# A router in two steps and the order of three small products in a four-layer kernel

## Chip, cores and metric

The kernel runs on one core of a Trainium2 chip. Times are microseconds of that core for one execution. The runs of the kernel before took 614.46, 614.35 and 614.35 us; their median, 614.35 us, is the time that the prediction is about.

## What is computed

The input x is 8 sequences of 256 tokens with 1024 features. Four layers follow, each added to its own input. The first is the one that the change is in: a dense matrix, a router that picks the best two of eight experts for each token, and their rank-16 adapters weighted by the router's gates. The reference, cut to its lines:

```python
# layer 0
base = einsum('btd,od->bto', x, W)
logits = einsum('btd,ed->bte', x, Wr) + 5.0 * one_hot(language_ids, E)[:, None, :]
topw, topi = top_k(logits, 2)
weights = softmax(topw, axis=-1)
gates = sum(one_hot(topi, E) * weights[..., None], axis=-2)
h = einsum('btd,erd->bter', x, A)
x = x + base + 2.0 * einsum('bter,bte,eor->bto', h, gates, B)
# layer 1: W, bias and a +-1 mask of each sequence, scaled by its coefficient
x = x + (x @ W1.T + b1) + (x @ (2 * mask - 1)) * coeff
# layer 2: one of eight matrices for each sequence
x = x + einsum('bsi,boi->bso', x, weight[ids])
# layer 3: one of eight rank-16 adapters for each sequence
x = x + einsum('bnr,bor->bno', einsum('bni,bri->bnr', x, B3[ids]), A3[ids])
```

## The kernel before, in words

**Precision.** Each fp32 operand is used as the sum of a high part (a cast to fp32r on ScalarE, `highs`, L288) and a low part (the operand less its high part, on VectorE, `lows`, L68). A product is then three matmuls: high by high, high by low, low by high. The adds of the residual (x + x W) are folded into the matrices, as an identity added to their diagonal blocks on GpSimd (L235).

**Stages.** The sequences are taken in pairs (512 tokens), and two pairs make a group. For each of the two groups g, layer 0 runs first, over both pairs at once, with Strassen's scheme in Winograd's form (seven products instead of eight; one place in the order of eight is used for expert products, below). Then layers 1 and 2 run pair by pair in 32 unit slots each, and layer 3 is spread as filler between them and the next group.

**Slots of layer 0.** Layer 0 has 16 slots, two for each entry of the product list. A slot s is issued by `l0_slot` (L786), always in this order:

1. stores and one load that is due;
2. `l0_evacuate` (L727), which takes finished accumulators out: at s = 6 ScalarE copies C11, in two halves (L734); at s = 8 VectorE makes V = accumulators + U1, in two halves (L736);
3. works listed under -s;
4. the high parts of the operands of the slot after the next (`highs`, ScalarE), then low parts of the next slot (`lows`, VectorE);
5. works listed under s in `l0_works` (L662);
6. TensorE's own work, `l0_main` (L759).

Each engine takes its instructions in the order in which these calls issue them. High parts live in five buffers and low parts in four, so the casts of a slot wait until TensorE has ended with an operand of an earlier slot. The accumulators of the products are four banks in two tiles. A new chain starts at slots 0, 6 and 10 in the same two tiles, so slot 6 has to wait for the copy of C11, and slot 8, which goes on in the accumulators that V reads, for V.

**The router.** For a pair p (p0 is the second of the group, p1 the first) it goes like this. `logits` (L301) multiplies x with the router's weights on TensorE, and ScalarE copies the result. `by_token` (L315) transposes it on TensorE. `router` (L323) is a row of small VectorE operations: the sum of four partial results, the bias, the best logit and its expert, the second best and its expert, their difference d; then ScalarE takes the exponential of d (L357), and VectorE turns it into the two weights and multiplies them into the one-hot rows. `expand` (L371) repeats each gate over the 16 ranks. `gates_by_rank` (L380) transposes that on TensorE, four matmuls, and ScalarE copies it (L389). `gate` (L398) multiplies it with the expert products h, which `experts` (L612) has made on TensorE. `split_gates` (L391) makes ghi (ScalarE, L394) and glo (VectorE). `lora` (L622) then adds the adapters' products to the accumulators: three matmuls for each of four blocks m.

In the first group, p0 has its logits and transposes in the first two slots. Its router and expansion are works of slot 2, its gate transposes are in the middle of slot 3, `gate` is in slot 4, and `split_gates` opens slot 5. Slots 4 and 5 hold the expert products of p1 in place of a Strassen product, and slot 5 ends with `lora` for p0. For p1 the logits are in the middle of slot 3, `by_token` at its end, router and expansion in slot 5, gate transposes in the middle of slot 6, and the rest in slot 8; `lora` runs again in slots 9, 13 and 15. In the second group the router has been run for both pairs at once in a slot of layer 2, before that group starts (`side`, L941), and only `expand` is left for slots 2 and 5.

The lines that a sentence can't give:

```python
        evacuate()                      # l0_slot, L795
        l0_evacuate(g, s)
...
        highs(f + HI_AHEAD)             # HI_AHEAD = 4, two operands per slot
...
        lows(f + LO_AHEAD)              # LO_AHEAD = 3
        for work in w.get(s, []):
            work()
...
        if s in (0, 6, 10):             # l0_main, L764
            chain(g, s)
...
            product(s, g, range(2), start=(s in (0, 6, 10)), lora=part, mid=mid)
```

Of the kernel before, what the change touches and what calls it, by code (L numbers as in the profile page):

```python
# [8 lines left out]
F32 = mybir.dt.float32  # L9
# [6 lines left out]
P = 128  # L16
# [18 lines left out]
def kernel(ctx: ExitStack, tc: tile.TileContext, x, lang, coeff, ids,  # L35
# [31 lines left out]
    def tt(o, a, b, op):  # L67
        nc.vector.tensor_tensor(o, a, b, op)  # L68
# [246 lines left out]
    def by_token(p):  # L315
        pts[p] = bank(1 - p % 2, f"pt{p}")
        lg = lgs.pop(p)
        for n in range(4):
            nc.tensor.transpose(pts[p][:, n * P:(n + 1) * P], lg[:, n * P:(n + 1) * P], ident)

    gxs = {}

    def router(pairs):  # L323
        n4 = 4 * len(pairs)
        t = lambda nm, w: gp.tile([P, n4, w], F32, tag=nm, name=nm)
        lv = t("lv", E)
        for i, p in enumerate(pairs):
            quarters = pts.pop(p).rearrange("p (n g e) -> p n e g", n=4, g=4)[:, :, :E, :]
            nc.vector.tensor_reduce(
                lv[:, 4 * i:4 * i + 4].rearrange("p n (e o) -> p n e o", o=1), quarters, AX.X,  # L330
                ALU.add)
        b0, nb = 2 * pairs[0], 2 * len(pairs)
        lv4 = lv.rearrange("p (b h) e -> p b h e", h=2)
        tt(lv4, lv4, bias[:, b0:b0 + nb].rearrange("p b (o e) -> p b o e", o=1)
           .to_broadcast([P, nb, 2, E]), ALU.add)
        revb = rev.to_broadcast([P, n4, E])

        def top(v, nm):
            mx = t(f"mx{nm}", 1)
            nc.vector.tensor_reduce(mx, v, AX.X, ALU.max)  # L340
            eq = t(f"eq{nm}", E)
            tt(eq, v, mx.to_broadcast([P, n4, E]), ALU.is_equal)
            tt(eq, eq, revb, ALU.mult)
            fi = t(f"fi{nm}", 1)
            nc.vector.tensor_reduce(fi, eq, AX.X, ALU.max)
            oh = t(f"oh{nm}", E)
            tt(oh, revb, fi.to_broadcast([P, n4, E]), ALU.is_equal)
            return mx, oh

        m1, oh1 = top(lv, "1")  # L350
        rest = t("rest", E)
        nc.vector.scalar_tensor_tensor(rest, oh1, -3.0e38, lv, ALU.mult, ALU.add)
        m2, oh2 = top(rest, "2")
        d = t("d", 1)
        tt(d, m2, m1, ALU.subtract)
        ex = t("ex", 1)
        nc.scalar.activation(ex, d, AF.Exp)  # L357

        den = t("den", 1)
        nc.vector.tensor_scalar(den, ex, 1.0, 0.5, ALU.add, ALU.mult)  # L360
        wt1 = t("wt1", 1)
        nc.vector.reciprocal(wt1, den)
        wt2 = t("wt2", 1)
        tt(wt2, wt1, ex, ALU.mult)
        tt(oh1, oh1, wt1.to_broadcast([P, n4, E]), ALU.mult)
        tt(oh2, oh2, wt2.to_broadcast([P, n4, E]), ALU.mult)
        tt(oh1, oh1, oh2, ALU.add)
        for i, p in enumerate(pairs):
            gxs[p] = oh1[:, 4 * i:4 * i + 4, :]

    def expand(p):  # L371

        gx = gp.tile([P, 4 * E, R], F32, tag="lg", name=f"gx{p}", bufs=3)
        nc.vector.tensor_copy(gx, gxs[p].rearrange("p n (e o) -> p (n e) o", o=1)
                              .to_broadcast([P, 4 * E, R]))
        gxs[p] = gx
# [3 lines left out]
    def gates_by_rank(p):  # L380

        pg = bank(1 - p % 2, f"pg{p}")
        gx = gxs.pop(p)
        for n in range(4):
            nc.tensor.transpose(pg[:, n * P:(n + 1) * P],
                                gx[:, n * E:(n + 1) * E, :].rearrange("p e r -> p (e r)"),
                                ident)
        gts[p] = gp.tile([P, N], F32, tag="lg", name=f"gt{p}", bufs=3)
        copy(gts[p], pg)  # L389
# [200 lines left out]
    def link(*args, **kw):  # L590

        mm(*args, skip_group_check=True, **kw)  # L592
# [29 lines left out]
    def lora(p, w):  # L622
        def part(m, o, stop=False):
            hi, lo = gates[p]
            link(o, w[0](m), hi, start=False, stop=False)
            link(o, w[0](m), lo, start=False, stop=False)
            link(o, w[1](m), hi, start=False, stop=stop)
        return part

    def lb_half(i):  # L630
# [31 lines left out]
    def l0_works(g):  # L662


        p0, p1 = pair_of(g, 0), pair_of(g, 1)
        w = {}

        def at(s, *fs):
            w.setdefault(s, []).extend(fs)

        def add(name, h, src):
            nc.gpsimd.dma_start(quad(g, name)[h], src, accum_op=ALU.add)

        def s1_add(h):
            fold_quad(quad(g, "S1")[h], h)
            add("S1", h, w0[1, 2 + h])

        def s3_add(h):
            t = quad(g, "S3")[h]
            copy(flat(t), flat(quad(g, "S2")[h]))  # L680
            fold_quad(t, h)
            add("S3", h, w0[1, 2 + h])

        def s4_add(h):
            copy(flat(quad(g, "S4")[h]), flat(quad(g, "S2")[h]))
            add("S4", h, w0[0, 2 + h])

        def less(h, name, j, i):

            t = flat(quad(g, name)[h])  # L690
            nc.scalar.mul(t, t, -1.0)  # L691
            add(name, h, x[pair_of(g, j)][:, 4 * i + 2 * h:4 * i + 2 * h + 2])

        def both(f, *args):
            return [lambda h=h: f(h, *args) for h in range(2)]

        def subs(o, a, b):
            return [lambda h=h: sub(g, o, a, b, h) for h in range(2)]

        def lb_parts():  # L700
            copy(lbs[0], lb_raw)
            tt(lbs[1], lb_raw, f32(lbs[0]), ALU.subtract)

        if g == 0:
            at(1, constants, *both(s1_add))
            at(2, *both(less, "T1", 1, 0), lambda: router([p0]), lambda: expand(p0))
            at(3, lb_parts, *subs("S2", "A11", "S1"))
            at(4, *both(s4_add), lambda: gate(p0))
            at(5, lambda: router([p1]), lambda: expand(p1))
        else:  # L710
            at(0, *both(s1_add), *both(less, "T1", 1, 0))
            at(2, lambda: expand(p0))
            at(3, *subs("S2", "A11", "S1"))
            at(4, *both(s4_add), lambda: gate(p0))
            at(5, lambda: expand(p1))
        at(-5, lambda: split_gates(p0, gts[p0]))
        at(4, *both(less, "T3", 1, 1))
        at(7, *subs("T2", "T1", "B22"))
        at(7, *both(s3_add))
        at(8, lambda: gate(p1), lambda: split_gates(p1, gts[p1]), lambda: gate_difference(g))  # L720
        for h in range(2):
            at(9 + h, lambda h=h: add("T4", h, x[p0][:, 4 + 2 * h:6 + 2 * h]))
        for i in range(4):
            at(12 + i, lambda i=i: split_c(p1, i))
        return w
# [20 lines left out]
    def l0_mids(g):  # L746


        p0, p1 = pair_of(g, 0), pair_of(g, 1)
        if g == 0:  # L750
            return {3: lambda: [gates_by_rank(p0), logits(p1)()], -3: lambda: by_token(p1),
                    6: lambda: gates_by_rank(p1)}
        mids = {0: lambda: proj_pair(1, 0), 1: lambda: rank_pair(1, 1, (0, 1)),
                2: lambda: gates_by_rank(p0), 6: lambda: gates_by_rank(p1)}
        mids.update({s: lambda: fill(2) for s in (3, 4, 5)})
        mids[-5] = lambda: fill(2)
        return mids
# [151 lines left out]
    def side(n):  # L909

        kind, q, m, j = slots[n]
        if kind == "L1":
            return
        u = pos[slots[n]] % 16
        b = 2 * q
        if q % 2 == 0:
            if u < 2:
                load_l3(b + u)
            if u in (4, 5):
                prep_l3(b + u - 4)  # L920
            if u in (2, 5, 8, 11):
                split_c(q + 1, u // 3)
            return
        l, p = ((9, 10), (11, 12)) if q == 1 else ((4, 5), (9, 10))
        if u in l:
            load_l3(b + u - l[0])
        if u in p:
            prep_l3(b + u - p[0])
        if q == 1:
            if u == 0:  # L930
                X[1] = region(GX[1], "x1", [P, 2, K, N], F32)
            if u in (1, 3, 5, 7):
                k = 4 * (u // 2 % 2)
                load_x(1, u // 4, k, k + 4)
            if u == 10:
                LA[1] = place_la(2)
                nc.sync.dma_start(LA[1], la)
            if u in (12, 13):
                la_parts(1, 4 * (u - 12), 4 * (u - 12) + 4)
            if u == 15:  # L940
                router([2, 3])  # L941

    def unit_slot(n):
        kind, q, m, j = slots[n]
# [169 lines left out]
```

## Time and profile before

| What | Value |
|---|---|
| median of 3 runs | 614.35 us |
| the profiled execution's own time | 613.21 us |
| its span in the profile | 611.0 us |
| mean granted TensorE clock | 0.994 |
| matmuls | 3244, busy 597.0 us |
| small products of the gates, layer 0, both groups | 32 with ghi and 16 with glo in each group |
| layer 0, first group, slots 2 to 15 | about 23 to 119 us |
| layer 0, second group | about 305 to 413 us |

Engines are PE (TensorE matmuls), PEld (its weight loads), DVE (VectorE), ACT (ScalarE), POOL (GpSimd) and SP (SyncE, which issues most DMAs). L12 is line 12 of the kernel. Tiles appear under the program's names: `whi` and `wlo` are high and low parts of operands, `mm` the accumulators of layer 0, `c` the blocks C11 to C22 and U1, V, W between them, `A` and `x` the Strassen operands, `pl`, `pt`, `pg`, `ph` the logits, their transposes, the gates' transposes and the expert products, `d` and `ex` the router's difference and its exponential, `gx` the expanded gates. The busy rows of the page show a slice of 15.3 us as one digit, in tenths, so that 9 means 90% or more. A wait is given as: engine, tile and line of the waiting instruction, what released it, then total us, number of times, and the longest. L68 is the helper of all two-operand VectorE work, and so is told apart by its tiles. Matmuls overlap: one of 512 columns is shown with 0.39 us but the next starts some 0.23 us after it, so positions are read from starts.

### The profile page before, as it was taken

What the parts mean: (1) busy time and instruction counts of PE and PEld (TensorE: products, weight loads), DVE (VectorE), ACT (ScalarE), POOL (GpSimd) and SP (SyncE); (2) the same over time, 40 slices, a digit from 0 to 9 for tenths busy, and PEclk for the clock granted to TensorE, in tenths of its full rate; (3) what the DMA queues carried; (4) which work ended last, traced back from release to release, by engine and by line L of the source; (5) the groups of instructions that cost most, each with busy time, mean ns of one, the idle gap of its engine ahead of it and who ended that gap; (6) DMA issues with size and microseconds to landing.
All of it is one profiled execution on the core that took longest, in us unless ns stands there. A gap on an engine that the chain in (4) does not pass through costs nothing.

```text
span 611.0 us, 8941 instructions
## 1 busy us (share of the span) xinstructions
PE 597.0 (98%) x3244; PEld 500.6 (82%) x3244; DVE 474.5 (78%) x555; ACT 385.1 (63%) x455; POOL 140.3 (23%) x174
## 2 busy tenths in 40 slices
PE   8997999999999999999999999999999999999995
PEld 7775788888888888888778778888888888888874
DVE  5576858899789999577656776879968999977752
ACT  4574656687678797554544746558866788864431
POOL 0320343014122213122210233511333111511000
PEclk9998999999999999999999999999999999999998
DMA  8986598267685767599940798935767686847404
GB/s 292 330 196 123 137 217 230 104 219 298 191 298 209 248 255 283 183 364 324 291 76 2 163 242 200 276 118 207 276 189 259 207 285 232 301 147 242 173 1 137
DMA packets 39389, 130.22 MB, mean 213 GB/s; under 512 B 4786, under 2 KB 6194, under 8 KB 38578
## 3 DMA queue, kind: packets, MB, share of 16 engines
q1 hardware_dynamic: 34594, 112.62, 52.6%
q0 software_dynamic: 4608, 16.78, 14.9%
q8 instruction: 25, 0.41, 0.3%
q10 hardware_dynamic: 144, 0.26, 0.1%
q14 instruction: 18, 0.15, 0.1%
HBM read 121.25 MB, written 8.39 MB: 212 GB/s over the span
## 4 chain that ended last, share of the span: by engine, by line
PE 92%; DVE 3%; ACT 2%; issue 1%; DMA 1%; ACTq 0%
PE po L524 38%; PE mm L592 27%; PE po L533 20%; PE pl L308 1%; DVE wlo L68 1%; PE pf L463 1%; PE pb L435 1%; ACT x L691 1%; PE ph L619 1%; PE ph L618 1%; PE ph L620 1%; ACT whi L288 1%; DMA x<-in_x 1%; DVE c L68 0%; PE pb L482 0%
## 5 line engine op out<-in xcount | busy, mean ns | idle before, releaser
L524 PE MATMUL po<-hl,whi 128*128 128x512 f32 x1016 | 254.5, 392 | 0.0
L524 PEld LDWEIGHTS po<-hl,whi 128*128 128x128 f32 x1016 | 182.7, 189 | 32.7
L68 DVE TENSOR_TENSOR wlo<-raw,whi 128x1024 fp32r<-128x1024 f32 x128 | 160.9, 1267 | 1.2 <-issue 1.1
L533 PEld LDWEIGHTS po<-hl,wlo 128*128 128x128 f32 x1016 | 137.6, 190 | 11.3 <-issue 1.6
L288 ACT CAST whi<-raw 128x1024 fp32r<-128x1024 f32 x128 | 133.7, 1048 | 18.0 <-PE mm L592 8.4
L533 PE MATMUL po<-hl,wlo 128*128 128x256 f32 x1016 | 142.3, 283 | 0.0
L592 PE MATMUL mm<-whi,whi 128*128 128x512 f32 x224 | 88.9, 397 | 5.1 <-ACT c L734 3.5
L592 PE MATMUL mm<-wlo,whi 128*128 128x512 f32 x224 | 88.2, 394 | 0.0
L235 POOL TENSOR_TENSOR raw<-raw,ident 128x128 f32<-128x128 f32 x72 | 59.2, 823 | 116.9 <-DMA raw<-in_w 86.9
L257 ACT ACTIVATE raw<-raw,negc,c 128x1024 f32<-128x1024 int32 x64 | 79.6, 1243 | 4.2 <-DMA raw<-in_mask 4.2
L592 PE MATMUL mm<-whi,wlo 128*128 128x512 f32 x224 | 71.7, 396 | 0.0
L235 POOL TENSOR_TENSOR w<-w,ident 128x128 f32<-128x128 f32 x28 | 34.6, 1237 | 158.3 <-DMA w<-in_w 134.1
L68 DVE TENSOR_TENSOR raw<-raw,w 128x1024 f32<-128x1024 f32 x56 | 69.3, 1237 | 1.5 <-POOL w L235 0.9
L68 DVE TENSOR_TENSOR wlo<-x,whi 128x1024 fp32r<-128x1024 f32 (+1 forms) x38 | 45.4, 1204 | 21.0 <-issue 10.3
L592 PEld LDWEIGHTS mm<-whi,whi 128*128 128x128 f32 x224 | 42.3, 189 | 17.6 <-ACT c L734 4.0
L592 PEld LDWEIGHTS mm<-whi,wlo 128*128 128x128 f32 x224 | 42.5, 190 | 9.9 <-DVE wlo L68 0.8
L592 PEld LDWEIGHTS mm<-wlo,whi 128*128 128x128 f32 x224 | 42.3, 189 | 8.7
L288 ACT CAST whi<-A 128x1024 fp32r<-128x1024 f32 x26 | 27.3, 1050 | 34.4 <-PE mm L592 16.9
L565 ACT COPY c<-po 128x512 f32<-128x512 f32 (+1 forms) x34 | 18.8, 552 | 47.0 <-PE po L533 47.0
L568 ACT ACTIVATE sum<-po,b_sb 128x512 f32<-128x512 f32 (+1 forms) x36 | 23.1, 642 | 31.6 <-PE po L533 31.6
L288 ACT CAST whi<-x 128x1024 fp32r<-128x1024 f32 x34 | 35.3, 1048 | 8.9 <-PE mm L592 8.9
L68 DVE TENSOR_TENSOR wlo<-A,whi 128x1024 fp32r<-128x1024 f32 (+1 forms) x30 | 35.8, 1193 | 4.7 <-ACT whi L827 2.7
(126 smaller groups left out, 523.6 us busy)
## 6 DMA issues: line engine op xcount, KB each, us to landing
raw<-in_mask SPq DMA_DIRECT2D x64, 512.0 KB, 5.5
raw<-in_w SPq DMA_DIRECT2D x64, 512.0 KB, 4.8
w<-in_w SPq DMA_DIRECT2D x28, 512.0 KB, 3.4
out<-c SPq DMA_DIRECT2D x31, 256.0 KB, 3.0
A<-in_w SPq DMA_DIRECT2D x14, 512.0 KB, 8.1
x<-in_x SPq DMA_DIRECT2D x6, 1024.0 KB, 7.8
A<-in_w POOLq DMA_DIRECT2D x12, 512.0 KB, 7.9
x<-in_x POOLq DMA_DIRECT2D x12, 512.0 KB, 8.5
```

The source lines that it names most:

```text
L68: nc.vector.tensor_tensor(o, a, b, op)
L235: (eng or nc.gpsimd).tensor_tensor(t, t, ident, ALU.add)
L257: nc.scalar.activation(f32(raws[n]), raws[n], AF.Identity, bias=negc[:, b:b + 1], scale=c2[:, b:b + 1])
L288: copy(prep_hi(i), flat(source(i)))
L308: mm(pl[c:c + 32, :], wrs[:, k, :], X[g][:, j, k, :], start=(k < 4), stop=(k >= 4))
L435: mm(pb[c:c + 32, j * T:(j + 1) * T], l3b[b][:, k, :], xts[b][:, k, :], start=(k < 4), stop=(k >= 4))
L463: mm(po[:, i * T:(i + 1) * T], at[:, (m + i) * P:(m + i + 1) * P], rt, start=True, stop=True)
L524: mm(po, hi[:, c], xhl[:, k, j].rearrange("p h t -> p (h t)"), start=(k == 0), stop=False)
L533: mm(po[:, :T], lo[:, c], xhl[:, k, j, 0, :], start=False, stop=(k == K - 1))
L565: copy(xs, po[:, :, T:])
L568: nc.scalar.activation(xs, po[:, :, T:], AF.Identity, bias=b1c)
L592: mm(*args, skip_group_check=True, **kw)
```

## The change

The router is cut in two at the difference d. `router` ends there and keeps d and the two one-hot tiles; the new `weigh` takes the exponential, the weights and the weighted gates. In the first group `weigh` and `expand` move one slot on (p0: from slot 2 to slot 3, ahead of that slot's other works; p1: from slot 5 to slot 6). The gate transposes of p1 move from the middle of slot 6 to the middle of slot 7; those of p0 stay in the middle of slot 3 but come after the logits of p1 instead of ahead of them. In the run of both second-group pairs `weigh` follows `router` at once. In `lora` the matmul with the gates' low part changes places with the one of the adapters' low part, and so comes third; it now carries the stop flag. This holds for both groups.

```diff
-    gxs = {}
+    gxs, routed = {}, {}
...
         d = t("d", 1)
         tt(d, m2, m1, ALU.subtract)
+        routed[tuple(pairs)] = d, oh1, oh2
+
+    def weigh(pairs):
+
+        n4 = 4 * len(pairs)
+        t = lambda nm, w: gp.tile([P, n4, w], F32, tag=nm, name=nm)
+        d, oh1, oh2 = routed.pop(tuple(pairs))
         ex = t("ex", 1)
         nc.scalar.activation(ex, d, AF.Exp)
...
             link(o, w[0](m), hi, start=False, stop=False)
-            link(o, w[0](m), lo, start=False, stop=False)
-            link(o, w[1](m), hi, start=False, stop=stop)
+            link(o, w[1](m), hi, start=False, stop=False)
+            link(o, w[0](m), lo, start=False, stop=stop)
...
-            at(2, *both(less, "T1", 1, 0), lambda: router([p0]), lambda: expand(p0))
-            at(3, lb_parts, *subs("S2", "A11", "S1"))
+            at(2, *both(less, "T1", 1, 0), lambda: router([p0]))
+            at(3, lambda: weigh([p0]), lambda: expand(p0), lb_parts, *subs("S2", "A11", "S1"))
             at(4, *both(s4_add), lambda: gate(p0))
-            at(5, lambda: router([p1]), lambda: expand(p1))
+            at(5, lambda: router([p1]))
+            at(6, lambda: weigh([p1]), lambda: expand(p1))
...
-            return {3: lambda: [gates_by_rank(p0), logits(p1)()], -3: lambda: by_token(p1),
-                    6: lambda: gates_by_rank(p1)}
+            return {3: lambda: [logits(p1)(), gates_by_rank(p0)], -3: lambda: by_token(p1),
+                    7: lambda: gates_by_rank(p1)}
...
                 router([2, 3])
+                weigh([2, 3])
```

## The prediction

> **What bounds the kernel now.** I read the page first, then who waits for whom on TensorE, then the chain around the longest such wait, then ScalarE's queue in that place, then the busy time in stretches of 3.41 us around it.
>
> ```profile
> PE 597.0 (98%) x3244; PEld 500.6 (82%) x3244; DVE 474.5 (78%) x555; ACT 385.1 (63%) x455; POOL 140.3 (23%) x174
> ...
> PE   8997999999999999999999999999999999999995
> ...
> PEclk9998999999999999999999999999999999999998
> ```
>
> TensorE is the bound, and only slices 3 and 4 (31 to 61 us) and the two ends leave anything: a 7 in its row, and just beside it an 8 in the granted clock.
>
> ```profile
> PE mm L592 <- ACT c L734: 3.5, 1, 3.5
> PE warm L987 <- POOL ident masks.py:199: 1.4, 1, 1.4
> PE pf L463 <- DVE c L68: 0.9, 2, 0.5
> PE mm L592 <- ACT whi L288: 0.6, 1, 0.6
> ...
> PE mm L592 <- DVE glo L68: 0.2, 1, 0.2
> ```
>
> One wait of 3.5 us stands out: a matmul waits for the copy of C11 (L734). The chain shows what the copy stood behind:
>
> ```profile
> 45.03 0.52 ACT ghi L394
> ...
> 46.26 2.27 DVE wlo L68 x2
> 48.53 0.21 DVE lv L329
> ...
> 51.42 0.08 DVE d L68
> 51.53 0.05 ACT ex L357
> 51.58 0.06 issue
> 51.64 1.00 ACT c L734
> 52.64 0.04 issue
> 52.69 4.61 PE mm L592 x12
> 57.30 0.44 PE pg L385 x4
> ```
>
> ScalarE's own queue (start, length, idle time before it, releaser) in the same place:
>
> ```profile
> 51.53 0.20 ACT L357 ACTIVATE ex<-d 128x4 f32<-128x4 f32 x1 [4.09 <-DVE d L68]
> 51.64 1.91 ACT L734 COPY c<-mm 128x1024 f32<-128x1024 f32 x2
> ```
>
> The reader is to see this: the exponential of the second router (slot 5) is ahead of slot 6's C11 copies on ScalarE, waits 4.09 us for VectorE's d, and TensorE, which ended slot 5 at 49.00, gets its accumulators back only at 52.69. The last view, three stretches (the columns after the length are busy us and instructions of PE, PEld, DVE, ACT, POOL, then granted clock, DMA share, GB/s):
>
> ```profile
> 50.29:53.70 3.41, 1.01 (x4) 0.86 (x5) 2.83 (x15) 2.17 (x4) 0.00 (x0) 1.00 1.05 197
> 53.70:57.11 3.41, 3.41 (x9) 2.54 (x8) 1.92 (x2) 1.74 (x2) 0.00 (x0) 0.50 0.42 82
> ...
> 603.24:606.65 3.41, 1.54 (x11) 1.28 (x9) 1.44 (x3) 1.20 (x4) 0.00 (x0) 1.00 0.24 89
> ```
>
> The edges 53.70 and 57.11 come from the clock in half-microsecond stretches (0.70 in the one from 53.5, 0.89 in the one from 57.0). After a stretch with 1.01 us of TensorE work the clock is granted at half for 3.41 us. So the wait is paid twice.
>
> **What the Trainium skill says.** (1) "TensorE: Matmul & The Clock Gate", Part 1: the clock falls to half after an idle window of about 3.4 us and comes back after a busy one. The trace agrees on length and ratio (3.41 us at 0.50), but the windows before a fall weren't idle: TensorE was busy for 1.01 us in one and 1.54 us (45%) in the other, at 603.24. (2) Same page, "Architectural detail": ScalarE and VectorE run strictly in order. The trace agrees: the first copy of C11 could start at 47.8, when block m=1 of slot 5's last product ended, and started at 51.64, behind the exponential. (3) "SBUF — State Buffer", "Who interferes with whom": a VectorE operation with two SBUF inputs contends with a GpSimd instruction that reads SBUF. The trace agrees: of the two T2 subtractions the one beside GpSimd's additions took 1.49 us, the other 1.22.
>
> **Part by part.** *The second router's exponential, weighting and expansion go from slot 5 to slot 6.* On ScalarE the C11 copies now follow the casts that end at 47.44, so they wait only for the adapter product of slot 5. *The low part last:* now that product's matmuls start at 45.59, then 46.32 (the second waits for glo, which ends at 46.26), and the remaining ten run 0.235 apart from 46.66. Afterwards the second uses the high part and starts at 45.82, the third waits for glo until 46.32: one matmul, 0.23 us, gets out of the wait, and the product ends at 48.77 instead of 49.00. Its block m=1 ends at 47.53, so the first copy runs 47.55 to 48.57 (1.02 us, the same copy in the second group, where no router stands there). That is before 48.77: the wait of 49.00 to 52.69, **3.69 us, goes**. The second copy ends near 50.0, needed at 51.5. Operands of slot 6 are there as now (the last low part ends at 48.53).
>
> *Slot 6.* It takes 52.69 to 60.34 now, 7.65 us; 24 matmuls at 0.2275 us (slot 7 shows this spacing) and 0.44 for the four gate transposes would be 5.90, so the half clock cost **1.75 us, which goes** with its cause. The transposes move on to slot 7, so slot 6 runs 48.77 to 54.23, and slot 7 takes 5.46 + 0.44 = 5.90, to 60.13.
>
> *What is late next: VectorE.* In slot 6 it ends d as now and is free at 51.42. Two low parts at 1.14 us apart follow, from 51.42 and 52.56 (slot 7 needs them at about 54.5 and 55.1, so they hold nothing up), then weighting and expansion at 53.70. They take 1.40 us (51.77 to 53.17 now); the exponential is behind two casts on ScalarE, which end near 52.1, so nobody waits for it, and the 0.27 us that VectorE waited for it now are saved. The expanded gates are there at 55.10; their transposes come at 57.0. Then VectorE does what it now does from 60.16: two low parts, two T2 subtractions, and the sum V, whose first half slot 8 needs because it writes the same accumulators. From the first low part to slot 8's first matmul this took 6.40 us here (60.16 to 66.56) and 6.18 in the second group (354.30 to 360.48). GpSimd's additions follow slot 6's end by 3.1 us now (60.34 to 63.47), so they will start at about 57.3, beside both subtractions instead of one: 6.18 + 0.27 = 6.45. Slot 8 starts at 55.10 + 6.45 = **61.55**. TensorE waits there 1.42 us, where it now waits 66.56 - 65.80 = 0.76: **0.66 us is given back**.
>
> *The first router's half goes from slot 2 to slot 3, and its transposes behind the next logits.* TensorE has no wait here now. The casts of slot 3 no longer stand behind the exponential and start when slot 2 ends, near 30.3; VectorE ends d at 31.2, does two low parts to 33.5 and the weighting to 34.95. The transposes are due at 34.34 + 1.85 = 36.2, after the logits: 1.25 us to spare. If that cover were gone, each microsecond would be one on the path. The lb and S2 work behind it ends at 38.3 instead of 38.65; slot 4 starts on TensorE's end of slot 3 anyway. Both orders have the same matmuls; I take 0, with 0.1 either way for the switch between shapes. No SP or GpSimd instruction is moved.
>
> *Second group.* Its router only gets split in two calls that follow each other: 0. The low part last saves 0.1 there in slot 5 (glo ends at 344.34, the second matmul could start at 344.25), but the next matmuls wait for VectorE (0.38 us at 347.60): 0. In slots 9, 13 and 15 no wait for glo shows: 0.
>
> **Sum.** 3.69 + 0.23 + 1.75 - 0.66 = **5.01 us** before slot 8 (66.56 to 61.55). From there to 593 us TensorE waits under 1.6 us in all now, and loads and buffers are released by its own progress, so I carry all of it to the end. The profiled execution took 613.21 (span 611.0, and 2.21 around it): 608.2. It lies 1.14 below the median of the runs, 614.35; from that I get 614.35 - 5.0 = **609.35**.
>
> **Unknown costs, both ends.** The clock after a 1.42 us wait: the window would hold at least 2.0 us of work (58%). The trace has a fall after 45% and none after 2.86 of 3.41 (84%, at 593.0), so this is not shown; 0 to +1.8, I take 0. GpSimd beside VectorE: -0.27 to +0.3. The S4 transfers, needed at 54.4 instead of 60.43: DMA is idle from 56.0 on, so they have landed by then; latest 1.6 us late at the cast, +0.85 behind VectorE's queue; they are the first two of four queued from 42.5 on, so I take 0.
>
> **Rivals.**
> A, as above: 609.35, own range 608.8 to 610.2. 66%.
> B, the new wait at slot 8 trips the clock: another 1.8 us at half speed, 611.15. For it: 45% did. Against: the wait can straddle two windows, and 58% is more. 15%.
> C, VectorE doesn't bind (V is ready when slot 7 ends): slot 8 starts at 60.13, gain 6.43, 607.9. Against: the second group shows VectorE's chain at the same place, 0.39 us of wait with nothing extra in it. 9%.
> D, the loads don't follow: the L1 mask loads start in slot 7 and DMA is 0.73 busy from 66 to 119 us; if they keep their old times, half the gain is lost by 119 us: 611.9 (range to 614.3). Against: their queue waits for low parts, that is for buffers. 7%.
> E, slower: the first router's expansion reaches TensorE late in slot 3, and the whole queue stands behind the four transposes at 36.2. At 4.2 us late, plus 1.8 for the clock, it is 609.35 + 6.0 = 615.35. It decides from 3.2 us late (gates at 39.4; 3.2 + 1.8 = 5.0). My time for the gates is 34.95, so 4.5 us of work would have to stand ahead that no row shows. 3%.
> That the edits don't do what they say has no room: the order in each queue is the order of the calls.
>
> **Numbers.** The range reaches from C to B with the bound of the clock, 607.9 to 611.5; D's worse half and E are left out. A change of 0.2% (1.2 us) is about what can be told from none. Faster by more: A, B, C and half of D, 0.94; within: 0.03; slower: 0.03.
>
> **What would show it.** Right: no wait for c L734 near 49; clock 1.00 in 50 to 58; slot 6 near 48.8; one wait of about 1.4 us near 60, released by VectorE's sum V; slot 8 near 61.5; all later stages 5 us earlier. Wrong: a wait at the transposes in slot 3 or 7, a half clock after 60, a wait for masks after 110.

## The result and the profile after

The changed kernel took 608.75 us (median of 6 runs, 607.83 to 610.38) against 614.32 (6 runs, 612.68 to 614.46): a ratio of 0.9919, 95% interval 0.9900 to 0.9937. This ratio isn't the quotient of the two medians: taken of 614.32 it is a gain of 5.0 us (3.9 to 6.1), while the medians are 5.6 apart. The forecast was 609.35. The profiled execution took 607.83 with a span of 605.6; before it was 613.21 with 611.0.

The page of the changed kernel, the same rows as before:

```profile
PE 594.8 (98%) x3244; PEld 499.7 (83%) x3244; DVE 474.9 (78%) x555; ACT 385.5 (64%) x455; POOL 139.2 (23%) x174
...
PE   8999999999999999999999999999999999999995
...
PEclk9999999999999999999999999999999999999999
```

The 7 in TensorE's row and the 8 beside it in the clock's are gone. TensorE's busy time fell by 2.2 us though it has the same 3244 matmuls: most of that is matmuls that the slow clock had stretched (1.5 us by the experiment with the filled wait, below). What TensorE waits for now:

```profile
PE mm L599 <- DVE c L68: 1.6, 2, 1.2
PE warm L996 <- POOL ident masks.py:199: 1.4, 1, 1.4
PE pf L470 <- DVE c L68: 1.2, 2, 0.6
PE mm L599 <- ACT whi L835: 0.3, 1, 0.3
```

The wait of 3.5 us for the copy of C11 has no successor of its size. Apart from the 1.4 us at the start of the kernel, which were there before, the longest is 1.2 us, for VectorE's sum V ahead of slot 8. ScalarE's queue in the same place:

```profile
47.24 1.02 ACT L742 COPY c<-mm 128x1024 f32<-128x1024 f32 x1
48.64 1.01 ACT L742 COPY c<-mm 128x1024 f32<-128x1024 f32 x1 [0.38 <-PE mm L599]
...
51.45 0.20 ACT L364 ACTIVATE ex<-d 128x4 f32<-128x4 f32 x1
```

The two copies of C11 now stand ahead of the exponential. The second waits for TensorE, as a copy should, and the exponential, which had stood 4.09 us at the head of the queue, finds its d ready. The chain of work through this stretch has moved to VectorE:

```profile
45.26 0.69 DVE glo L68
45.95 2.27 DVE wlo L68 x2
...
51.03 0.06 DVE d L68
...
51.10 2.35 DVE wlo L68 x2
...
54.78 2.35 DVE wlo L68 x2
57.13 2.80 DVE x L68 x2
59.93 1.15 DVE c L68
61.08 0.14 issue
61.22 2.99 PE mm L599 x12
```

From glo to slot 8's first matmul it is VectorE without a break, and TensorE is off the chain. Last, the clock's two windows around the new wait (columns as in the prediction; how their edges are found is in the last section):

```profile
58.01:61.42 3.41, 2.20 (x10) 1.55 (x9) 3.41 (x4) 1.92 (x3) 2.63 (x4) 1.00 0.69 173
61.42:64.84 3.42, 3.42 (x16) 2.81 (x16) 3.42 (x4) 0.16 (x1) 0.88 (x1) 1.00 1.01 184
```

The first holds the whole wait and 2.20 us of TensorE work, and the clock stays at 1.00 behind it.

**A common zero.** Executions differ in when the first loads land: the start of glo in slot 5, before which these kernels differ by no more than the first router's place, lies at 45.57 before and 45.26 after, and at up to 47.07 in the experiments. So positions are given below as time after glo's start.

| | slot 6 starts | slot 8 starts | first slot of layer 1 |
|---|---|---|---|
| before | 7.12 | 20.99 | 73.38 |
| after | 3.18 | 15.96 | 68.34 |
| gained | 3.94 | 5.03 | 5.04 |

The 5.03 us won by slot 8 is neither added to nor lost later: layer 1 of the second group starts 367.3 after glo before and 362.3 after it now.

### The profile page after: what moved, and what is told of

The parts are those of the page before. It is cut to its first block, busy times and chain, and to the rows that moved or that the text cites. A ratio compares the mean times of both kernels' runs of the same rounds, so it can differ in the third digit from the quotient of the medians.

```text
span 605.6 us, 8939 instructions
## 1 busy us (share of the span) xinstructions
PE 594.8 (98%) x3244; PEld 499.7 (83%) x3244; DVE 474.9 (78%) x555; ACT 385.5 (64%) x455; POOL 139.2 (23%) x174
## 4 chain that ended last, share of the span: by engine, by line
PE 91%; DVE 4%; ACT 2%; issue 1%; DMA 0%; ACTq 0%
PE po L531 39%; PE mm L599 25%; PE po L540 20%; DVE wlo L68 2%; PE pl L308 1%; PE pf L470 1%; PE pb L442 1%; DVE x L68 1%; DVE c L68 1%; ACT x L698 1%; PE ph L626 1%; PE ph L625 1%; PE ph L627 1%; DMA x<-in_x 0%; PE pb L489 0%
## 5 line engine op out<-in xcount | busy, mean ns | idle before, releaser
L288 ACT CAST whi<-raw 128x1024 fp32r<-128x1024 f32 x128 | 133.7, 1048 | 18.0 <-PE mm L599 8.4
L235 POOL TENSOR_TENSOR w<-w,ident 128x128 f32<-128x128 f32 x28 | 36.0, 1287 | 163.7 <-DMA w<-in_w 107.4
L288 ACT CAST whi<-A 128x1024 fp32r<-128x1024 f32 x26 | 27.3, 1051 | 34.9 <-PE mm L599 15.3
L288 ACT CAST whi<-x 128x1024 fp32r<-128x1024 f32 x34 | 35.3, 1049 | 10.8 <-PE mm L599 8.8
```

Source lines behind the costliest of these rows:

```text
L235: (eng or nc.gpsimd).tensor_tensor(t, t, ident, ALU.add)
L288: copy(prep_hi(i), flat(source(i)))
```

## The experiments

The theory: ScalarE's in-order wait for d, with the copy of C11 behind it, cost the wait and a half-clock window; with it gone, VectorE sets the start of slot 8. The rivals: that the gain came from where the weighting and the transposes stand, or from the low part's place, or from the first router's move; and that slot 6 was slow for another reason than the clock.

### Only the second router's part

```diff
-            at(2, *both(less, "T1", 1, 0), lambda: router([p0]))
-            at(3, lambda: weigh([p0]), lambda: expand(p0), lb_parts, *subs("S2", "A11", "S1"))
+            at(2, *both(less, "T1", 1, 0), lambda: router([p0]), lambda: weigh([p0]),
+               lambda: expand(p0))
+            at(3, lb_parts, *subs("S2", "A11", "S1"))
...
-            return {3: lambda: [logits(p1)(), gates_by_rank(p0)], -3: lambda: by_token(p1),
+            return {3: lambda: [gates_by_rank(p0), logits(p1)()], -3: lambda: by_token(p1),
...
-            link(o, w[1](m), hi, start=False, stop=False)
-            link(o, w[0](m), lo, start=False, stop=stop)
+            link(o, w[0](m), lo, start=False, stop=False)
+            link(o, w[1](m), hi, start=False, stop=stop)
```

> The changed kernel with only the second router's part left: weighting and expansion in slot 6, its transposes in slot 7; the first router is whole again in slot 2 with its transposes ahead of the logits, and the low part is second again. Theory (the exponential that holds up the copy of C11 is all that counts, and VectorE sets the start of slot 8): the product of slot 5 ends 0.23 us later, slot 6 starts near 48.7 instead of 48.44, slot 8 still near 61.2, and the time is that of the changed kernel, 608.8 within 0.3. Rival (the low part's place and the first router's move each bring a part of it): slot 8 near 61.6 or later, and 609.2 or more.

Measured: 607.96 us (607.66 to 608.55), ratio 0.9905 (0.9883 to 0.9927). Slot 6 starts 3.43 after glo's start, 0.25 later than in the changed kernel, and slot 8 at 15.94 against 15.96. What TensorE waits for:

```profile
PE mm L599 <- DVE c L68: 1.4, 2, 1.0
...
PE mm L599 <- DVE glo L68: 0.2, 1, 0.2
```

The 0.2 us for glo is back, and the wait for V is shorter by the same amount. So the whole gain at slot 8 is the second router's. The low part's place and the first router's move, taken together, bring nothing there, since VectorE sets slot 8 either way.

### An exponential that is ready

```diff
-        nc.scalar.activation(ex, d, AF.Exp)
+        early = c2[:, :4].rearrange("p (n o) -> p n o", o=1)
+        nc.scalar.activation(ex, early if list(pairs) == [0] else d, AF.Exp)
```

> The kernel before, but the second router's exponential in the first group reads a constant that is ready early instead of d, so the gates of that pair are other numbers; all instructions and their order stay. Theory (ScalarE's wait for d, with the C11 copies queued behind it, is the cause): no wait near 49 to 52, slot 6 near 49.0, clock 1.00, VectorE's chain as before from 55.2, slot 8 near 61.4, 609.3. Rival (the gain comes from where VectorE's weighting and the transposes stand, not from ScalarE's queue): the wait before slot 6 stays or moves to the transposes in slot 6, and the time stays within 1.2 us of 614.3.

Measured: 610.03 us (609.41 to 611.52), ratio 0.9938 (0.9919 to 0.9958); slot 8 at 16.65, so 4.34 of the 5.03 us. TensorE's waits:

```profile
PE pg L386 <- DVE gx L375: 1.0, 1, 1.0
...
PE mm L593 <- DVE c L68: 0.8, 2, 0.4
PE mm L593 <- DVE glo L68: 0.2, 1, 0.2
```

With every instruction in its old place, and only the input of one exponential changed, the wait for the copy of C11 is gone and most of the gain is there. The rival falls. But the expectation was 0.7 us too good: with slot 6 starting early, its transposes now come before the expanded gates, and TensorE waits 1.0 us in the middle of the slot. Moving the transposes on avoids that wait.

### The transposes back in slot 6

```diff
-                    7: lambda: gates_by_rank(p1)}
+                    6: lambda: gates_by_rank(p1)}
```

> The changed kernel with the second pair's gate transposes back in the middle of slot 6. Theory (TensorE takes its queue in order, and the expanded gates are only there near 54.8): TensorE waits in the middle of slot 6 from 51.2 to 54.8, slot 6 ends near 58.0, VectorE's low parts wait for that, and slot 8 starts near 64.3 with a full clock and near 65.8 with a half clock after the wait: 611.9 to 613.4. Rival (the transposes' place is of no weight): 608.8.

Measured: 613.37 us (20 runs, 611.13 to 615.78), ratio 0.9989 (0.9978 to 1.0000); slot 8 at 20.52. TensorE's longest wait, and two stretches of 3.41 us:

```profile
PE pg L392 <- DVE gx L381: 3.6, 1, 3.6
```

```profile
54.41:57.82 3.41, 1.19 (x7) 1.07 (x8) 2.03 (x8) 0.50 (x1) 0.00 (x0) 1.00 0.56 108
57.82:61.23 3.41, 3.41 (x10) 2.62 (x9) 0.21 (x1) 0.09 (x1) 0.00 (x0) 0.50 0.01 1
```

The old wait is back at another instruction, 3.6 us for the gates instead of 3.5 for the copy, and the half clock follows it (1.19 us of work in the window before). Splitting the router without moving what reads its result would have been worth 0.5 us at slot 8. The rival falls clearly.

### The wait filled with matmuls

```diff
+        if (g, s) == (0, 6):
+            idle = bank(2, "idle")
+            for _ in range(14):
+                mm(idle, lbs[0][:, :P], lbs[0][:, :N], start=True, stop=True)
         if s in (0, 6, 10):
             chain(g, s)
```

> The kernel before, with 14 matmuls of 512 columns into an unused bank ahead of slot 6, about 3.2 us, so that TensorE is busy while it waits for the copy of C11; their result is not used. Theory (half of the harm beyond the wait is the clock): the copy comes when it came, slot 6 starts at 52.7, the clock stays at 1.00 and slot 6 takes 5.9 instead of 7.65, so slot 8 starts near 64.8 and the time falls by 1.75 to 612.6. Rival (slot 6 is slow for another reason, or VectorE sets slot 8 anyway): slot 8 stays at 66.5, 614.3.

Measured: 611.90 us (15 runs, 611.23 to 613.06), ratio 0.9967 (0.9956 to 0.9978). Slot 6 starts at 7.12, exactly as before, and slot 8 at 19.45 against 20.99. Slot 6 in this kernel, from its first matmul to slot 7's:

```profile
52.92:59.03 6.11, 6.11 (x28) 5.00 (x29) 3.08 (x5) 3.34 (x4) 0.00 (x0) 1.00 0.35 68
```

and in the kernel before:

```profile
52.69:60.34 7.65, 7.65 (x28) 6.09 (x29) 3.08 (x5) 3.34 (x4) 0.00 (x0) 0.78 0.31 60
```

The same 28 matmuls take 1.54 us less at a clock of 1.00 than at a mean of 0.78, and slot 8 is earlier by the same 1.54. So useless work in a wait that stays as long as it was makes the kernel faster by 2.0 us (interval 1.4 to 2.7; the positions show 1.54 of it). The clock's part is shown, at 1.5 rather than 1.75: at full clock too the first two matmuls after the wait start 0.35 us apart instead of 0.23, and slot 6 takes 6.11 us, not the 5.90 that the forecast compared with.

### Only the low part last

```diff
-            link(o, w[0](m), lo, start=False, stop=False)
-            link(o, w[1](m), hi, start=False, stop=stop)
+            link(o, w[1](m), hi, start=False, stop=False)
+            link(o, w[0](m), lo, start=False, stop=stop)
```

> The kernel before with only the low part last. Theory (slot 6's start is set by the exponential, so what slot 5's product saves is lost in the wait): slot 6 starts 7.12 us after glo's start as before, with a wait 0.2 us longer, and 614.1 stays within 0.4. Rival (the order of the three products brings a part of the gain by itself): slot 6 starts 0.2 or more earlier, 613.8 or less.

Measured: 614.88 us (14 runs), ratio 1.0007 (0.9991 to 1.0023); slot 6 at 7.12, slot 8 at 20.97. Slot 6's first matmul:

```profile
54.19 0.50 PE L592 MATMUL mm<-whi,whi 128*128 128x512 f32 x1 [3.77 <-ACT c L734]
```

The wait is 3.77 instead of 3.53 us: what slot 5's product saves, the wait takes.

### VectorE's chain lengthened

```diff
-        at(7, *subs("T2", "T1", "B22"))
+        at(7, *subs("T2", "T1", "B22"), *([subs("T2", "T1", "B22")[1]] if g == 0 else []))
```

> The changed kernel with the second half of T2 computed twice in slot 7 of the first group (the same numbers again). Theory (VectorE's chain sets slot 8 one for one): the wait before slot 8 grows from 1.2 to about 2.5 us, slot 8 starts near 17.3 us after glo's start, and the time rises by 1.3, or by 3.0 if a window with so little work trips the clock. Rival (VectorE has slack there): no change from 608.8.

The changed kernel again, on the same chip:

> The changed kernel once more, on the same chip as the others. Theory: 608.3 to 609.3, slot 8 starts 15.95 us after glo's start with a wait near 1.2, clock 1.00 behind it. The rival that the new wait trips the clock in some executions would show a half clock in the 3.4 us after slot 8's start in this one.

Measured: the changed kernel 608.93 us (608.01 to 611.11), slot 8 at 15.96, wait 1.24, clock 1.00 behind it. With the doubled subtraction 612.19 us (9 runs, 611.13 to 614.29), slot 8 at 17.42 and a wait of 2.71:

```profile
60.00:63.41 3.41, 0.70 (x4) 0.34 (x3) 3.38 (x4) 1.93 (x2) 3.00 (x4) 1.00 0.70 119
63.41:66.82 3.41, 3.41 (x10) 2.64 (x9) 3.41 (x4) 0.00 (x0) 0.36 (x1) 0.50 0.95 163
```

One more subtraction lengthens VectorE's work on T2 from 2.81 to 4.27 us and moves slot 8 by the same 1.46 us, and in this execution the wait of 2.7 us trips the clock. Together the medians differ by 3.3 us.

### VectorE's chain shortened

```diff
-        at(7, *subs("T2", "T1", "B22"))
+        at(7, subs("T2", "T1", "B22")[0])
...
-        at(8, lambda: gate(p1), lambda: split_gates(p1, gts[p1]), lambda: gate_difference(g))
+        at(8, lambda: gate(p1), lambda: split_gates(p1, gts[p1]), lambda: gate_difference(g),
+           subs("T2", "T1", "B22")[1])
```

> The changed kernel with the second half of T2 made at the end of slot 8's works instead of slot 7's, in both groups, so that VectorE comes to the sum V one subtraction of 1.4 us earlier. Theory (after the change VectorE's chain through V sets slot 8): the wait of 1.2 us before slot 8 goes almost wholly, slot 8 starts 14.7 us after glo's start instead of 15.96, the second group's 0.4 us goes too, and the time is 1.2 to 1.6 below the changed kernel's, near 607.3. Rival (something else is as late, the end of slot 7's products or the four transposes in it): slot 8 moves by less than 0.5, 608.6.

> The kernel just above with the gates' low part second again, as before the change. Theory (the low part's place saves TensorE 0.23 us in slot 5, which only shows once VectorE no longer sets slot 8): slot 8 starts 0.2 us later than in the kernel just above, 607.5. Rival (the order is of no weight there either): the same start within 0.05 us.

Measured: 606.59 us (605.86 to 609.03), ratio 0.9890 (0.9867 to 0.9913); slot 8 at 14.59, 1.37 earlier than in the changed kernel. VectorE's two halves of V:

```profile
58.56 1.21 DVE L68 TENSOR_TENSOR c<-mm,c 128x1024 f32<-128x1024 f32 x1
60.14 1.22 DVE L68 TENSOR_TENSOR c<-mm,c 128x1024 f32<-128x1024 f32 x1 [0.37 <-PE mm L599]
```

Now VectorE waits for TensorE (0.37 us ahead of the second half), and TensorE no longer waits for V in either group. With the low part second again it is 607.33 us (606.65 to 608.63), and slot 8 starts at 14.79: 0.20 later. The low part's place is worth its 0.2 us as soon as VectorE isn't the later of the two. The medians' 0.7 us is more than these positions show; the ranges overlap.

### The gates' high part ahead of T3

The same kernel was run once more beside a version of it:

```diff
-        at(-5, lambda: split_gates(p0, gts[p0]))
-        at(4, *both(less, "T3", 1, 1))
+        at(-5, lambda: split_gates(p0, gts[p0]), *both(less, "T3", 1, 1))
```

> The changed kernel with the second half of T2 made in slot 8, once more, beside the next one. 606.6 within 0.7.

> The kernel of the run just above, with the two negations of T3 (2.0 us of ScalarE) moved from slot 4's works to behind the gates' high part at the start of slot 5, in both groups. Theory (in slot 5 too it is ScalarE's order that makes TensorE wait, for ghi and glo: 0.5 us in the first group, little in the second): ghi is ready 1.9 us earlier, the waits for ghi and glo go, slot 8 starts 0.5 us earlier counted from the start of the expert products, and the time falls by 0.5 to 606.1. Rival (the casts that then stand later on ScalarE, or the later T3 transfer, hold up what follows): no gain or a loss, 606.6 or more.

Measured: 607.67 us (606.18 to 609.74) and 606.80 (605.03 to 608.60); ratios to the kernel before 0.9877 (0.9854 to 0.9900) and 0.9870 (0.9846 to 0.9895). The first is 1.1 us above the 606.59 of the same kernel before, more than the 0.7 allowed for; the times don't separate the two. In the traces, counted from slot 4's first expert product (glo itself is moved here), slot 8 starts at 20.10 instead of the 20.37 and 20.38 in the two traces of the kernel without it: 0.27 us, half of what was expected, and the wait for glo is gone. In the profiled execution of 607.67's kernel TensorE waited at a place where only one other trace has a wait (1.0 us, that of the doubled subtraction):

```profile
PE pt L319 <- ACT lg L312: 1.5, 1, 1.5
```

There ScalarE's copy of the second group's logits was late behind a cast that waited 2.7 us for a load (2.4 in that other trace, 0.8 to 2.3 in the eleven without such a wait). It is once more a wait at the head of ScalarE's queue, and may be a part of the scatter between executions.

## Why the prediction was right, step by step

- **Wait for the copy of C11** (3.69 us, and 0.23 for the low part). Right: slot 6 starts 3.94 us earlier, 3.92 forecast. The cause is shown by the ready exponential: the wait goes when nothing but that exponential's input changes.
- **Half clock in slot 6** (1.75). The cause is right, shown by the filled wait and again by the transposes put back; the size is 1.54. The forecast compared slot 6 with an undisturbed slot and named the clock for all of the difference; but slot 6 after a wait takes 6.11 us at full clock, while slot 7 of the changed kernel, with the same 28 matmuls and no wait ahead of it, takes 5.92. In the changed kernel slot 6 follows without a gap, so both parts are gained: it took 5.49, 5.46 forecast. The number held, then, with a fifth of a microsecond in it for which the forecast had no reason.
- **VectorE is late next** (slot 8 at 61.55, a wait of 1.42, 0.66 given back). Right: in the profile the wait is 1.21, against 0.62 before, so 0.59 is given back; measured from start to start, as the forecast did, it is 1.37 against 0.76. (The list of waits of the kernel before puts the 0.62 down to a cast, whi L288. But that cast ended at 66.58, after slot 8's first matmul had started at 66.56, while V's first half had ended at about 66.42; in the filled kernel the same 0.62 is put down to V.) From VectorE's first low part to slot 8 it took 6.44 us, 6.45 forecast with both T2 subtractions beside GpSimd's additions (1.48 each, 2.81 for the pair in the trace, 2.55 in the second group). Lengthening and shortening VectorE's chain moved slot 8 one for one until TensorE was the later.
- **The low part last** was listed with 0.23 us. It is true of slot 5 and worth nothing at slot 8, where the sum let VectorE decide; the forecast said so only by its 0.66 given back. The run without it shows no gain at slot 8 from it.
- **The first router's move** (0). Right: the expanded gates were there at 34.9, forecast 34.95, a microsecond ahead of their transposes.
- **The moved transposes** were taken as 0.44 us that changes slot. The forecast didn't price leaving them: in slot 6 they bring back a 3.6 us wait and the half clock, 4.6 of the 5.0 us.
- **No loss later**, against the rival that loads would keep their times: right, the gain at slot 8 is there at the second group's layer 1.
- **The clock after the new wait** (rival, 15%): in the two profiled executions of the changed kernel it stays at 1.00. The forecast's argument that the wait can straddle two windows wasn't what saved it: in both executions the wait lay whole in one, with 2.20 and 2.17 us of work (64%). The forecast had a closer case in its own trace than the 84% it named: the window ahead of the one with 1.01 us, 46.88 to 50.29, held 2.28 us (67%), and the clock stayed at 1.00 behind it.

The sum before slot 8 was 5.01 forecast and is 5.03. The time, 608.75, is 0.6 below 609.35, which lies within the scatter of the runs.

## What to carry to other kernels

When the bound engine waits for a cheap copy, look at what stands at the head of the copy's queue: an instruction there that waits for a third engine delays everything behind it. Moving it back one stage cost nothing here, because its readers moved with it. After such an edit find the engine that is late next by adding up its queue from the last release; here that gave the remaining wait to 0.2 us, and one more subtraction moved out of that queue won another 1.4 at slot 8. A wait on TensorE should be priced with the clock that it costs, and with no gain for whatever only shortens the work ahead of it.

## What was not expected of the hardware

The Trainium skill ("TensorE: Matmul & The Clock Gate", Part 1) ties the fall of the clock to an idle window. Here the windows ahead of a fall were often far from idle, and the traces show how much work is enough.

First, where the windows lie. In the four traces with a fall in the middle (the kernel before, the transposes back in slot 6, only the low part last, the doubled subtraction) the clock comes back after 3.41 us, and falls once more at the end of the kernel, 549.5, 549.5, 553.0 and 539.3 us after it came back: 161, 161, 162 and 158 times 3.4133 us. So the windows of a trace follow one another without gaps, and in a trace whose clock falls only at the end they can be counted back from that fall. In the changed kernel it falls at 604.14, and 159 windows earlier an edge lies at 61.42.

Then the work in each window, in all thirteen traces after their first 11 us. Every window with 1.64 us of TensorE work or less was followed by one at half clock (0.54, 0.70, 1.01, 1.19, 1.54, 1.61, 1.62 and 1.64 us among them). Every window with 1.78 us or more was not (1.78, 1.80, 2.07, 2.11, 2.17 and so on). The two nearest to each other, with the window that follows, from the second execution of the changed kernel and from the one with the ready exponential:

```profile
598.03:601.44 3.41, 1.64 (x12) 1.35 (x10) 1.53 (x3) 1.20 (x4) 0.00 (x0) 1.00 0.21 77
601.44:604.85 3.41, 0.00 (x0) 0.00 (x0) 0.00 (x0) 0.00 (x0) 0.00 (x0) 0.50 0.73 230
```

```profile
599.44:602.86 3.42, 1.78 (x12) 1.48 (x10) 1.67 (x3) 1.20 (x4) 0.00 (x0) 1.00 0.16 61
602.86:606.27 3.41, 0.00 (x0) 0.00 (x0) 0.00 (x0) 0.00 (x0) 0.00 (x0) 1.00 0.77 246
```

It is the same work at the end of the kernel in both, laid a little differently over the windows. So in these traces the limit lies between 48% and 52% of a window, counted in TensorE's busy time as the profile shows it (the ends of matmuls are modelled there).

An estimate from this: among dense matmuls a wait of up to about 1.6 us (3.41 less 1.78) leaves every window above the limit, and the 1.2 us of the changed kernel is such a wait. A longer one trips the clock only if more than that falls into one window. The 2.7 us of the doubled subtraction lay whole in the window from 60.00 to 63.41; shared evenly by two windows they would leave 2.06 us in each.
